# Later due times for layer-norm scalings in a planned graph kernel, and the last store in two pieces

## The chip, the cores and the metric

The kernel runs on one core of one Trainium2 chip. The metric is the device time of one execution in microseconds (us). A core has five engines that run side by side, each with its own in-order queue of instructions: TensorE (PE, matrix products), VectorE (DVE, elementwise work and statistics), ScalarE (ACT, activations and copies), GpSimd (POOL) and SyncE (SP, which here only issues transfers). They wait for one another through semaphores. Products land in PSUM banks, which PE writes and ACT and DVE read; everything else lies in SBUF or in DRAM.

## The reference, cut to what matters

Sixteen graphs (batches) of 1024 nodes with 128 features share one symmetric 0/1 adjacency matrix. Layer 0 is a graph attention, layer 1 five steps of a gated recurrent unit, and each ends with a residual and a layer norm:

```python
h = x @ others_weight                       # layer 0: attention
e = leaky(u1[:, idx1] + u2[:, idx2])
att = softmax(where(adj > 0, e, NEG_BIG), axis=1)
y = layernorm(x + att @ h + x @ self_weight)

h = y                                       # layer 1: five steps
for step in range(5):
    m = adj @ h                             # the reference takes it twice: m_in, m_out
    u3 = h @ u3_w.T + u3_b
    z = sigmoid([m, m] @ w3_w.T + w3_b + u3)
    r = sigmoid([m, m] @ w4_w.T + w4_b + u3)
    hv = tanh([m, m] @ w5_w.T + w5_b + (r * h) @ u5_w.T + u5_b)
    h = (1 - z) * h + z * hv
out = layernorm(y + h)
```

A layer norm subtracts the mean over the 128 features and divides by sqrt(variance + 1e-5).

## The kernel before, in words

The adjacency matrix stays in SBUF (`adj`), with four tables of sums of its quarters (`tab`). Batches are taken in pairs. `layer0(b)` computes the attention of one batch and its norm; the result `y0` is the start of layer 1 and is also put away in DRAM (`yd`) for the residual at the end. `messages(q, s, k)` multiplies the state of pair q by the adjacency matrix in step s. Where a step is in the list `PLAIN`, it does so with plain products (PE rows `ps_acc`); otherwise it needs seven products in place of eight, on sums of quarters (rows `ps_acc_a`, `ps_acc_c` and `gz` of line 621). The accumulated bank `ps_acc_a` is copied out by ACT between two products that go on adding to it (lines 1141 and 1143), so PE can't start the next one ahead of that copy. `gates(b, s, soon)` does the gates: u3 (L1189), a copy of it (L1192), r and z (L1199, and tanh on ACT, L1202), r times h (DVE, L1209), the candidate (L1215, L1216, tanh L1221), and the new h by three DVE instructions (L1224, L1227, L1230). Each batch's 1024 nodes are worked on in two halves, e or g = 0 and 1.

After a step, `leave(b, s)` turns h from feature-major to node-major: DVE transposes blocks of 32x32 (L579), SP sends the tile to DRAM with the blocks swapped (L589) and reads it back as `G` or `F` (L597). ACT and DVE then split it into a high and a low part (L609, L613). After the last step of batches 0 to 13 it adds the residual (L1332, into a tile of kind `o`, of which there are two), norms it in place, and POOL issues the store to the output (L1344). SP has loaded the residual into that tile before (L1324). The last two batches, 14 and 15, end in `end(b, s, g, h, rank)`: PE transposes h (L571), DVE adds the residual (L1262), and SP stores the result (L1278), half a batch at a time.

`layernorm(...)` has three parts. `look` is DVE's: statistics of four blocks of 128 features (L527, L529). `power` is POOL's: variance plus epsilon, to the power -0.5 (L533, L534), and the product with the mean (L539 and L540, or L542 and L543 for batches with the other sign). `scale` is ACT's: four activations of 128x128 with that scale and bias (L548). With `short=True`, which only batch 15's second half uses, POOL stops after the power (for this sign) and DVE scales (`scale_short`, L554). The norms of layer 0 are called `y`, those of layer 1 `o`, in the tile names too (`mv_y`, `rstd_o`).

Nothing of this is issued in the order of the source. Each piece of work is added to a `Plan` with its engine, a length in ns, a rank, and what it reads and writes. `Plan.order` then plays a list schedule: of the pieces that are ready on a free engine it takes the one with the lowest rank. A piece becomes ready when all that it depends on have ended in the plan, plus a lag; lengths on DVE and ACT are taken 1.1 times. The lag is set by the engine (200 ns for POOL) or by the piece itself. The order found so is the order in which instructions go into the engines' queues; on the chip each queue keeps it, and the semaphores do the rest. So a lag in the plan costs no time by itself: it moves the dependent instruction, and then whatever the plan finds to do in its place.

```python
plan.add("POOL", 2301 if short else 3001, rank, power, reads=[(mv, 0)], writes=[(rstd, 0)])
if short:
    dve(900, rank, scale_short, reads=[*after, (mv, 0), (rstd, 0)], writes=[write])
else:
    act(1250, rank, scale, reads=[*after, *later, (mv, 0), (rstd, 0)], writes=[write])
```

The argument `later` names further things that the scaling has to follow in the plan. Before, only batch 14's second half has one: the tanh result `hv` of batch 15, last step, second half.

Of the kernel before, what the change touches and what calls it, by code (L numbers as in the profile page):

```python
# [16 lines left out]
P = 128  # L17
# [3 lines left out]
STEPS = 5  # L21
# [116 lines left out]
def kernel(  # L138
# [79 lines left out]
    def exact(pools):  # L218
# [300 lines left out]
                dve(V, 1 + c / 4, sum_, reads=[*y, *more], writes=[(("tab",), c, n)])  # L519


        def layernorm(key, g, rank, after, src, dst, write, sg=1, short=False, later=()):
            stats, mv, rstd = ("stats", *key, g), ("mv", *key, g), ("rstd", *key, g)

            def look():
                for j in range(4):
                    nc.vector.bn_stats(T(stats)[:, j, :], src(j))  # L527
                for j in range(4):
                    nc.vector.bn_aggr(T(mv)[:, j, :], T(stats)[:, j, :])  # L529

            def power():
                mean, var, r = T(mv)[:, :, 0], T(mv)[:, :, 1], T(rstd)
                nc.gpsimd.tensor_scalar(r[:, 0, :], var, EPS, None, ALU.add)  # L533
                nc.gpsimd.tensor_tensor(r[:, 0, :], r[:, 0, :], mhalf[:, 0:4], ALU.pow)  # L534
                if short:
                    if sg < 0:
                        nc.gpsimd.tensor_scalar(r[:, 0, :], r[:, 0, :], -1.0, None, ALU.mult)
                elif sg > 0:
                    nc.gpsimd.tensor_scalar(r[:, 1, :], mean, -1.0, None, ALU.mult)  # L539
                    nc.gpsimd.tensor_tensor(r[:, 1, :], r[:, 1, :], r[:, 0, :], ALU.mult)  # L540
                else:
                    nc.gpsimd.tensor_tensor(r[:, 1, :], mean, r[:, 0, :], ALU.mult)  # L542
                    nc.gpsimd.tensor_scalar(r[:, 0, :], r[:, 0, :], -1.0, None, ALU.mult)  # L543

            def scale():
                r = T(rstd)
                for j in range(4):
                    nc.scalar.activation(  # L548
                        dst(j), src(j), AF.Identity, bias=r[:, 1, j : j + 1], scale=r[:, 0, j : j + 1]
                    )  # L550

            def scale_short():
                for j in range(4):
                    nc.vector.tensor_scalar(  # L554
                        dst(j), src(j), T(mv)[:, j, 0:1], T(rstd)[:, 0, j : j + 1], ALU.subtract, ALU.mult
                    )

            after = after if isinstance(after, list) else [after]
            dve(1100, rank, look, reads=after, writes=[(stats, 0), (mv, 0)])
            plan.add("POOL", 2301 if short else 3001, rank, power, reads=[(mv, 0)], writes=[(rstd, 0)])  # L560
            if short:
                dve(900, rank, scale_short, reads=[*after, (mv, 0), (rstd, 0)], writes=[write])
            else:
                act(1250, rank, scale, reads=[*after, *later, (mv, 0), (rstd, 0)], writes=[write])

# [65 lines left out]
        def layer0(b):  # L631
# [331 lines left out]
            for g in range(2):  # L963
                rank = rank0(b) + D["l5"]

                def y(g=g):
                    return T(yT[g])

                t = ("ps", "t", b, "y", g)
                if on_pe(b, "y"):  # L970
                    transposes(y, [(yT[g], 0)], t, rank)
                else:
                    k, d, t = (x + (b, "y", g) for x in (("T",), ("D",), ("F",)))
                    turn(k, y, [(yT[g], 0)], rank)
                    away(k, d, rank)
                    back(d, t, rank)

                def src(j, t=t, flat=on_pe(b, "y")):
                    return T(t)[:, j * P : (j + 1) * P] if flat else chunks(T(t))[:, j]

                def dst(j, g=g, flat=on_pe(b, "y")):
                    c = T(y0[g])[:, j, :]
                    return c if flat else c.rearrange("p (a j) -> p a j", a=4)

                layernorm(("y", b), g, rank0(b) + D["l6"], (t, 0), src, dst, (y0[g], 0), sign(b))

            if not plain(b // 2, 0):

# [256 lines left out]
        def end(b, s, g, h, rank):  # L1245

            hT, t = ("hT", b), ("ps", "t", b, s, g)
            o, yd = ("y0" if b == B - 1 else "o", b, "o", g), ("yd", b, g)
            sp(
                450,  # L1250
                rank,
                lambda: nc.sync.dma_start(T(o).rearrange("p c d -> p (c d)"), T(yd)),
                reads=[(yd, 0), (("m", b, s, 0), 0)],
                writes=[(o, "y")],
                lag=2300,
            )

            transposes(h, [(hT, g)], t, rank + D["tr"])

            def add_():  # L1260
                x = T(o).rearrange("p c d -> p (c d)")
                nc.vector.tensor_tensor(x, T(t), x, ALU.add)  # L1262

            dve(V, rank + D["o"], add_, reads=[(t, 0), (o, "y")], writes=[(o, "raw")])

            def src(j):
                return T(o)[:, j, :]

            def dst(j):
                return T(o)[:, j, :]  # L1270


            later = [(("hv", B - 1, STEPS - 1, 1), 0)] if (b, g) == (B - 2, 1) else []
            layernorm(("o", b), g, rank + D["ln"], (o, "raw"), src, dst, (o, 0), sign(b), b == B - 1 and g == 1, later)
            sp(
                450,
                rank + D["out"],
                lambda: nc.sync.dma_start(out[b].rearrange("(c p) d -> p c d", p=P)[:, 4 * g : 4 * g + 4, :], T(o)),  # L1278
                reads=[(o, 0)],
            )  # L1280

        def leave(b, s):

# [2 lines left out]
            for g in range(2):  # L1286

                def h(g=g):
                    return T(hT)[:, g * HALF : (g + 1) * HALF]

                k, d = ("T", b, s, g), ("X", b, s + 1, g)
                if s < STEPS - 1 and on_pe(b, s):
                    t = ("ps", "t", b, s, g)
                    transposes(h, [(hT, g)], t, rank + D["tr"])
                    split(
                        ("blk", b, "h", s + 1, g),
                        lambda t=t: T(t).rearrange("p (c a j) -> p c a j", c=4, a=4),
                        [(t, 0)],
                        rank_of(b, s + 1),
                    )  # L1300
                    continue
                if s < STEPS - 1:
                    turn(k, h, [(hT, g)], rank + D["tr"])
                    away(k, d, rank + D["tr"])
                    continue

                if b >= B - 2:
                    end(b, s, g, h, rank)
                    continue

                t = ("ps", "t", b, s, g)
                if on_pe(b, s):
                    transposes(h, [(hT, g)], t, rank + D["tr"])
                else:
                    t = ("F", b, s, g)
                    turn(k, h, [(hT, g)], rank + D["tr"])
                    away(k, d, rank + D["tr"])
                    back(d, t, rank + D["o"])

                o, yd = ("o", b, g), ("yd", b, g)  # L1320
                sp(
                    450,
                    rank + D["o"],
                    lambda o=o, yd=yd: nc.sync.dma_start(T(o).rearrange("p c d -> p (c d)"), T(yd)),  # L1324
                    reads=[(yd, 0), (hT, g)],
                    writes=[(o, "y")],
                )

                def last(t=t, o=o, flat=on_pe(b, s)):
                    x = T(o).rearrange("p c (a j) -> p c a j", a=4)  # L1330
                    n = T(t).rearrange("p (c a j) -> p c a j", c=4, a=4) if flat else chunks(T(t))
                    nc.vector.tensor_tensor(x, n, x, ALU.add)  # L1332

                dve(V, rank + D["o"], last, reads=[(t, 0), (o, "y")], writes=[(o, "raw")])

                def at(j, o=o):
                    return T(o)[:, j, :]

                layernorm(("o", b), g, rank + D["ln"], (o, "raw"), at, at, (o, 0), sign(b))
                plan.add(  # L1340
                    "POOL",
                    900,
                    rank + D["out"],
                    lambda o=o, g=g: nc.gpsimd.dma_start(  # L1344
                        out[b].rearrange("(c p) d -> p c d", p=P)[:, 4 * g : 4 * g + 4, :], T(o)
                    ),
                    reads=[(o, 0)],
                    writes=[((o, "sent"), 0)],
                    lag=2600,
                )  # L1350
# [347 lines left out]
```

## Time and profile before

| what | us |
|---|---|
| median of three runs | 1460.33 |
| lowest and highest run | 1458.93, 1460.43 |
| the profiled execution, its own time | 1468.01 |
| its span, first to last instruction | 1466.2 |
| PE not busy: up to 40 us | 3.1 |
| PE not busy: 100 to 200 us | 1.3 |
| PE not busy: 200 to 400 us | 4.4 |
| PE not busy: 400 to 600 us | 2.2 |
| PE not busy: 1200 to 1400 us | 1.3 |
| PE not busy: from 1440 us on | 14.4 of 27.0 |

The idle rows come from the view of busy time by stretches; the stretches that are left out have none. A row of the timeline gives start, duration, engine, line of the kernel, operation, tiles, shape, and in brackets the idle time of the engine before it with what ended that. Lines of the profile are lines of the kernel before. Busy times of PE are modelled ends of pipelined products, so one group's end overlaps the next one's start a little. In PE's rows a product of 32-bit numbers shows as two instructions.

### The profile page before, as it was taken

How to read it: one execution, taken by the hardware profiler on the slowest of the kernel's cores; microseconds unless marked ns; L12 is line 12 of the kernel's file. 1: busy time of each engine (PE TensorE's matmuls, PEld its weight loads, DVE VectorE, ACT ScalarE, POOL GpSimd, SP SyncE). 2: the span in 40 equal slices, each digit the busy share in tenths (PEclk: the TensorE clock that was granted, in tenths of full speed). 3: DMA queues.
4: the chain of work that ended last, by engine and by line, in shares of the span. 5: the costliest groups of instructions: out<-in, count | busy, mean ns of one | idle time of the engine just before them, and what ended most of it. 6: DMA issues, size and time to landing. Idle time of an engine off the chain costs nothing.

```text
span 1466.2 us, 17789 instructions
## 1 busy us (share of the span) xinstructions
PE 1440.4 (98%) x5020; PEld 902.3 (62%) x5020; DVE 1160.1 (79%) x2753; ACT 896.2 (61%) x1792; POOL 203.3 (14%) x323
## 2 busy tenths in 40 slices
PE   9999999998999999999999999999999999999996
PEld 7766656665566656666666656656566656556663
DVE  5997789868888789987888788896988877776535
ACT  5656465665657665666657576566655656664544
POOL 0311001012101150110201112011200123000201
PEclk9999999999999999999999999999999999999998
DMA  7426135554434643455434543445432554223201
GB/s 250 145 55 205 52 102 150 137 158 116 112 100 137 184 126 90 121 163 150 108 108 123 158 129 101 115 143 159 123 89 79 150 166 129 58 72 87 72 0 31
DMA packets 188032, 174.20 MB, mean 119 GB/s; under 512 B 34239, under 2 KB 137366, under 8 KB 187926
## 3 DMA queue, kind: packets, MB, share of 16 engines
q1 hardware_dynamic: 182562, 156.41, 37.8%
q0 software_dynamic: 4800, 15.73, 3.2%
q8 instruction: 41, 0.67, 0.2%
q10 hardware_dynamic: 564, 0.85, 0.2%
q14 instruction: 65, 0.53, 0.1%
HBM read 95.68 MB, written 77.24 MB: 118 GB/s over the span
## 4 chain that ended last, share of the span: by engine, by line
PE 88%; DVE 4%; DMA 2%; SPq 1%; ACT 1%; issue 1%; POOL 1%; DVEq 0%; POOLq 0%; ACTq 0%
PE ps_acc_a L621 16%; PE ps_g_r L1199 8%; PE ps_g_v L1215 8%; PE ps_g_v L1216 8%; PE gz L1199 8%; PE ps_g_r L1189 8%; PE ps_acc_c L621 8%; PE ps_acc_po L621 8%; PE ps_acc L621 5%; PE gz L621 4%; PE ps_g_ph L658 1%; PE ps_idle L419 1%; SPq L589 1%; PE ps_acc_px L925 1%; PE ps_acc_po L939 1%
## 5 line engine op out<-in xcount | busy, mean ns | idle before, releaser
L1215 PE MATMUL ps_g_v<-m,wm 128*128 128x512 f32 x320 | 163.5, 592 | 0.1
L1216 PE MATMUL ps_g_v<-r,u5h 128*128 128x512 f32 x320 | 163.4, 592 | 0.0
L1199 PE MATMUL ps_g_r<-m,wm 128*128 128x512 f32 x320 | 160.0, 593 | 2.6 <-ACT gz L1192 2.6
L1199 PE MATMUL gz<-m,wm 128*128 128x512 f32 x320 | 159.5, 592 | 0.0
L1189 PE MATMUL ps_g_r<-hT,u 128*128 128x512 f32 x320 | 153.3, 592 | 0.0
L1224 DVE TENSOR_TENSOR hv<-hv,hT 128x512 f32<-128x512 f32 x160 | 109.8, 686 | 51.5 <-ACT hv L1221 51.0
L621 PE MATMUL ps_acc_a<-tab,blk_s 128*128 128x512 f32 x544 | 148.6, 415 | 1.6 <-ACT m L1141 1.6
L1209 DVE SCALAR_TENSOR_TENSOR r<-r,hT 128x512 f32<-128x512 f32 x160 | 109.2, 685 | 51.3 <-ACT r L1202 51.0
L1202 ACT ACTIVATE r<-ps_g_r,bh 128x512 f32<-128x512 f32 x160 | 109.1, 687 | 66.4 <-PE ps_g_r L1199 66.1
L621 PE MATMUL ps_acc_po<-adj,blk 128*128 128x512 f32 x512 | 141.5, 423 | 0.0
L1202 ACT ACTIVATE z<-gz,bh 128x512 f32<-128x512 f32 x160 | 109.6, 687 | 24.5 <-PE gz L1199 24.0
L621 PEld LDWEIGHTS ps_acc_a<-tab,blk_s 128*128 128x128 f32 x544 | 101.1, 188 | 37.5 <-issue 11.1
L621 PEld LDWEIGHTS ps_acc_po<-adj,blk 128*128 128x128 f32 x512 | 95.9, 188 | 36.6 <-issue 12.5
L1230 DVE SCALAR_TENSOR_TENSOR hT<-hv,hT 128x512 f32<-128x512 f32 x160 | 108.7, 681 | 2.2
L1227 DVE SCALAR_TENSOR_TENSOR hv<-z,hv 128x512 f32<-128x512 f32 x160 | 108.4, 678 | 2.1 <-ACT z L1202 1.1
L1192 ACT COPY gz<-ps_g_r 128x512 f32<-128x512 f32 x160 | 91.0, 572 | 29.7 <-PE ps_g_r L1189 28.2
L533 POOL TENSOR_SCALAR rstd_y<-mv_y 128x4 f32<-128x4 f32 x32 | 13.5, 422 | 682.1 <-DVE mv_y L529 657.6
L1216 PEld LDWEIGHTS ps_g_v<-r,u5h 128*128 128x128 f32 x320 | 60.6, 189 | 76.8 <-issue 61.1
L1199 PEld LDWEIGHTS gz<-m,wm 128*128 128x128 f32 x320 | 60.5, 190 | 76.4 <-issue 76.4
L621 PE MATMUL ps_acc<-adj,blk_h 128*128 128x512 f32 x384 | 101.3, 414 | 0.0
L609 ACT CAST blk_s<-G 128x512 fp32r<-128x512 f32 x136 | 82.3, 617 | 30.8 <-DVE G L1083 29.2
L613 DVE TENSOR_TENSOR blk_s<-G,blk_s 128x512 fp32r<-128x512 f32 x136 | 92.0, 681 | 8.7 <-ACT blk_s L609 8.2
(191 smaller groups left out, 2595.4 us busy)
## 6 DMA issues: line engine op xcount, KB each, us to landing
G<-X SPq DMA_DIRECT2D x140, 256.0 KB, 2.9
X<-T SPq DMA_DIRECT2D x552, 64.0 KB, 1.8
yd<-y POOLq DMA_DIRECT2D x32, 256.0 KB, 3.3
D_y<-T_y SPq DMA_DIRECT2D x112, 64.0 KB, 1.8
F_y<-D_y SPq DMA_DIRECT2D x28, 256.0 KB, 2.7
X<-y SPq DMA_DIRECT2D x28, 256.0 KB, 2.0
D_b<-T_b SPq DMA_DIRECT2D x112, 64.0 KB, 2.2
F_b<-D_b SPq DMA_DIRECT2D x28, 256.0 KB, 3.0
```

The source lines that it names most:

```text
L613: lambda: nc.vector.tensor_tensor(half(1), src(), half(0), ALU.subtract),
L621: nc.tensor.matmul(T(bank), T(blk)[:, k, c, :], right(c), start=(first and i == 0), stop=(last and i == len(terms) - 1), skip_group_check= ...
L1189: nc.tensor.matmul(T(pr), u3, h(), start=True, stop=True)
L1192: nc.scalar.copy(T(pz), T(pr))
L1199: nc.tensor.matmul(T(p_), wm[:, j, :], T(m), start=False, stop=True, skip_group_check=True)
L1202: nc.scalar.activation(T(t), T(p_), AF.Tanh, bias=bh[:, j : j + 1], scale=0.5 * sg)
L1209: lambda r=r, h=h: nc.vector.scalar_tensor_tensor(T(r), T(r), 1.0, h(), ALU.add, ALU.mult),
L1215: nc.tensor.matmul(T(pv), wm[:, 2, :], T(m), start=True, stop=False)
L1216: nc.tensor.matmul(T(pv), u5h, T(r), start=False, stop=True)
L1224: nc.vector.tensor_tensor(T(hv), T(hv), h(), ALU.subtract)
L1227: nc.vector.scalar_tensor_tensor(T(hv), T(z), 1.0, T(hv), ALU.add, ALU.mult)
L1230: nc.vector.scalar_tensor_tensor(h(), T(hv), 0.5, h(), ALU.mult, ALU.add)
```

## The change

It has four parts.

1. `layernorm` takes an argument `calm`, which it hands to the plan as the lag of POOL's power. For the `y` norms it is 1201 ns for batches 4 to 15; for the `o` norms of batches 0 to 13 (in `leave`) 4001 ns. Elsewhere it stays None, which means 200 ns.
2. `later` now holds for both halves of batch 14: the first half's scaling follows the tanh of batch 15's first half in the plan, the second half's that of the second half.
3. `scale_short` is cut into two pieces of two instructions each, every one a piece of the plan of its own.
4. The last store (batch 15, second half) becomes two of 128 KB each: ACT's queue issues the first, SP's queue the second, each after its own piece of the scaling.

Ranks (`D` and the rest) are the same in both kernels. Numbers and kinds of instructions are the same too, but for one more transfer on ACT's queue, as the last store is two.

```diff
-        def layernorm(key, g, rank, after, src, dst, write, sg=1, short=False, later=()):
+        def layernorm(key, g, rank, after, src, dst, write, sg=1, short=False, later=(), calm=None):
...
-            def scale_short():
-                for j in range(4):
+            def scale_short(js):
+                for j in js:
...
-            plan.add("POOL", 2301 if short else 3001, rank, power, reads=[(mv, 0)], writes=[(rstd, 0)])
+            plan.add(
+                "POOL", 2301 if short else 3001, rank, power, reads=[(mv, 0)], writes=[(rstd, 0)], lag=calm
+            )
             if short:
-                dve(900, rank, scale_short, reads=[*after, (mv, 0), (rstd, 0)], writes=[write])
+                for i in range(2):
+                    js = range(2 * i, 2 * i + 2)
+                    dve(
+                        510,
+                        rank,
+                        lambda js=js: scale_short(js),
+                        reads=[*after, (mv, 0), (rstd, 0)],
+                        writes=[(write[0], i)],
+                    )
...
-                layernorm(("y", b), g, rank0(b) + D["l6"], (t, 0), src, dst, (y0[g], 0), sign(b))
+                layernorm(("y", b), g, rank0(b) + D["l6"], (t, 0), src, dst, (y0[g], 0), sign(b), calm=1201 if b >= 4 else None)
...
-            later = [(("hv", B - 1, STEPS - 1, 1), 0)] if (b, g) == (B - 2, 1) else []
+            later = [(("hv", B - 1, STEPS - 1, g), 0)] if b == B - 2 else []
...
-            sp(
-                450,
-                rank + D["out"],
-                lambda: nc.sync.dma_start(out[b].rearrange("(c p) d -> p c d", p=P)[:, 4 * g : 4 * g + 4, :], T(o)),
-                reads=[(o, 0)],
-            )
+            view = out[b].rearrange("(c p) d -> p c d", p=P)[:, 4 * g : 4 * g + 4, :]
+            if (b, g) == (B - 1, 1):
+                for i, (add, by) in enumerate(((act, nc.scalar), (sp, nc.sync))):
+                    cs = slice(2 * i, 2 * i + 2)
+                    add(450, rank + D["out"], lambda by=by, cs=cs: by.dma_start(view[:, cs], T(o)[:, cs]), reads=[(o, i)])
+            else:
+                sp(450, rank + D["out"], lambda: nc.sync.dma_start(view, T(o)), reads=[(o, 0)])
...
-                layernorm(("o", b), g, rank + D["ln"], (o, "raw"), at, at, (o, 0), sign(b))
+                layernorm(("o", b), g, rank + D["ln"], (o, "raw"), at, at, (o, 0), sign(b), calm=4001)
```

## The prediction

> **What bounds the kernel now.** I read the head of the page first, then the waits of TensorE (PE), then the timeline around the longest of these waits, then busy time by stretches, and last the timeline of the final 20 us.
>
> ```profile
> span 1466.2 us, 17789 instructions
> PE 1440.4 (98%) x5020; PEld 902.3 (62%) x5020; DVE 1160.1 (79%) x2753; ACT 896.2 (61%) x1792; POOL 203.3 (14%) x323
> ```
>
> PE is busy 98% of the span, and the change leaves each of its instructions in place by kind and number. So only the 26 us in which PE is not busy can be won, and any new idle time of PE is lost. Who makes PE wait (total, times, longest, in us):
>
> ```profile
> PE ps_acc_a L621 <- ACT m L1143: 4.4, 1, 4.4
> PE ps_t L571 <- DVE hT L1230: 3.0, 3, 1.5
> PE ps_g_r L1199 <- ACT gz L1192: 2.6, 2, 1.7
> ...
> PE ps_acc_a L621 <- ACT m L1141: 1.6, 2, 1.1
> ```
>
> The L571 row belongs almost wholly to the end of the kernel. The three rows that name ACT are single events. The largest, in the timeline (start, duration, engine, line, operation; in brackets the idle time before it and its releaser):
>
> ```profile
> 332.12 1.27 DVE L613 TENSOR_TENSOR blk_x<-G,blk_x 128x512 fp32r<-128x512 f32 x2
> ...
> 332.30 4.78 POOL L533 TENSOR_SCALAR rstd_o<-mv_o 128x4 f32<-128x4 f32 x1 [29.03 <-DVE mv_o L529]
> ...
> 336.91 0.71 DVE L579 STREAM_TRANSPOSE T<-hT 128x512 f32<-128x512 f32 x1
> ...
> 338.57 0.24 POOL L543 TENSOR_SCALAR rstd_o<-rstd_o 128x4 f32<-128x4 f32 x1
> 338.85 1.65 ACT L548 ACTIVATE o<-o,rstd_o 128x128 f32<-128x128 f32 x4 [5.46 <-POOL rstd_o L543]
> ...
> 340.97 0.58 ACT L1143 ACTIVATE m<-ps_acc_a 128x512 f32<-128x512 f32 x1
> ...
> 341.60 3.59 PE L621 MATMUL ps_acc_a<-tab,blk_x 128*128 128x512 f32 x8 [4.37 <-ACT m L1143]
> ```
>
> The power of a layer norm (POOL, L533 to L543) is ready 6.6 us after its statistics (331.84+0.37 to 338.57+0.24). The planner had reckoned 3.0 + 0.2 us, so it had put the scaling L548 early in ACT's queue; ACT stands there 5.46 us, the copy L1143 is queued behind it, and PE waits for that copy. POOL's timeline shows two more slow L533: 4.18 us at 521.63 (ACT then idles 3.45 us, PE 1.72 us) and 2.99 us at 538.74 (PE 0.52 us at 547.2). Its shortest is 0.215 us. The stall costs more than its length:
>
> ```profile
> 330.00:337.20 7.20, 7.20 (x24) 3.84 (x22) 6.84 (x18) 2.27 (x4) 4.81 (x2) 1.00 0.20 50
> 337.20:341.60 4.40, 0.03 (x1) 0.00 (x0) 1.01 (x3) 2.75 (x7) 2.26 (x4) 1.00 0.47 151
> 341.60:345.30 3.70, 3.70 (x9) 2.92 (x10) 3.63 (x10) 1.24 (x4) 0.04 (x1) 0.54 0.29 84
> ```
>
> The last column but two is PE's granted clock. After the stall it is 0.54: the eight products at 341.60 take 3.59 us, where groups of eight in the chain of waits take 1.86. That is 1.7 us more.
>
> **What the Trainium skill says.** "SBUF — State Buffer", section "Who interferes with whom": a DVE instruction with two inputs in SBUF and a GpSimd instruction that reads SBUF contend for one port pair, and the loser blocks. The trace agrees and goes further: L533 starts at 332.30, sits through the eight two-input DVE instructions from 332.12 on, and ends just after the one-input transpose L579 begins. The two others also end with such a transpose. "TensorE: Matmul & The Clock Gate", Part 1: an idle window of about 3.4 us halves the clock. The trace agrees: 0.54 after 4.37 us, and no such stretch after the stall of 1.72 us. "DMA: Bandwidth & Descriptors", section "Issuing engines are not separate DMA queues": a second issuing engine saves only issue time. The trace can't test that.
>
> **The change part by part.**
>
> *Powers reckoned later.* For the `o` norms of batches 0 to 13 the planner now reckons 3.0+4.0 = 7.0 us, for the `y` norms of batches 4 to 15 3.0+1.2 = 4.2. This adds no instruction; it moves L548 back in ACT's queue, and with it everything planned after. I compared the emitted orders: PE's is the same up to about 260 us, different until about 1383 us, and the same again after. I anchored ACT's and DVE's instructions to PE's order, since PE hardly ever waits. The three scalings that stalled then stand 6.9, 1.6 and 11 us of PE work further behind their statistics, and none of these statistics is followed directly by a two-input DVE instruction any more (before: eight, seven, five). So I expect all three stalls gone: 4.37+1.7 (clock), 1.72, 0.52; sum 8.3 us. From below: the second may survive in part. The covers: ACT is 61% busy and has other work to put in place of the scaling; a store waits for its scaling (63.2 us on POOL, all hidden) and is sent up to 4 us later. On POOL a power queued behind such a store waits with it; on SP the load L1324 waits for the store that frees its `o` buffer (48.8 us in total, up to 8.2), with the transfers L589 and L597 behind it. The planner has moved these too, so I take 0, up to 2 us if not.
>
> *New stalls.* Before, I count 15 powers with five or more two-input DVE instructions right behind their statistics; three came late. After there are 13, so about 13×3/15 = 2.6 that come late. Eight of the 13 are `o` norms, nearly all covered by 7.0 us (slowest seen 6.7). Five are `y` norms: about one slow. The worst new one is that of batch 8, second half: eight such instructions at 0.60 us each plus the 1.8 us for the rest gives 6.6 us against 4.2, so ACT is up to 2.4 us late. PE lost 4.37, 1.72 and 0.52 of 5.46, 3.45 and 4.49 us that ACT lost, so about half: 1.2. With small stalls of other kinds (1.10 at 1205.9 is there now) I add 1.5 us; from 0 to 6.
>
> *Both scalings by the last tanhs.*
>
> ```profile
> 1447.25 1.64 ACT L548 ACTIVATE o_o<-o_o,rstd_o 128x128 f32<-128x128 f32 x4
> ...
> 1449.36 0.67 ACT L1221 ACTIVATE hv<-ps_g_v,b 128x512 f32<-128x512 f32 x1
> ...
> 1450.95 0.69 ACT L1221 ACTIVATE hv<-ps_g_v,b 128x512 f32<-128x512 f32 x1 [0.93 <-PE ps_g_v L1216]
> ...
> 1459.67 1.12 DVE L554 TENSOR_SCALAR y_o<-y_o,mv_o,rstd_o 128x128 f32<-128x128 f32 x4 [1.72 <-POOL rstd_o L534]
> 1459.91 1.43 SPq L1278 DMA_DIRECT2D out_dram<-y_o  x2
> ```
>
> The first half's scaling moves from ahead of the first tanh to between the two. The first tanh's bank is ready at 1449.20 (1448.18+1.02), so it gains at most 0.12. The second starts at about 1449.87+1.5 = 1451.4 in place of 1450.95, 0.4 late; but DVE reaches its result only at 1452.19 (now 1452.07), and the tanh then ends at 1452.09. Sum: -0.1, at worst +0.4. The second half's scaling stays behind both tanhs. Stores of batch 14 go out before 1454 and are hidden.
>
> *Last store in two.* The same four L554; after the second (about 1460.25) ACT can send 128 KB, 0.55 us before SP's store at 1460.81; after the fourth SP sends the rest. One more DMA on ACT: behind it are only ACT's flag load (0.46 us) and branch. The DMA view of the last 8 us shows data flowing at 260 to 300 GB/s from 1460.8 to 1463.2 with one dip to 123, so the gain is the dip and a shorter tail: -0.2; from -0.9 (all of issue and dip) to +0.4 (a further queue to wait for).
>
> **Sum.** Against the profiled execution (1468.01: span 1466.2 and 1.8 around it): -8.3 + 1.5 - 0.1 - 0.2 = -7.1, giving 1460.9. The median of the runs is 1460.33, 7.7 us below that execution. PE's work is the same in each, so some of its idle time may be missing from ordinary runs: between all of the 6.8 us net and nothing may count there. I take two thirds, because the DVE runs that block POOL lie in the program's order, while how far DVE lags behind depends on the landing of data (3.33 us of waiting for F before this one). So -4.5 - 0.3 = -4.8: **1455.5**.
>
> **Rivals.**
> *A, forecast*: 1455.5; 0.55. Within it 0.47 faster, 0.08 same.
> *B, the stalls are the profiled execution's own*: the 7.7 us speak for it, the lock's fixed order against it. Left are 0.3 from the end and some 0.5 of small stalls: 1459.5; 0.22 (0.19 same, 0.02 faster, 0.01 slower).
> *C, slower*: the lock moves to `y` norms that are reckoned at only 4.2 us, at batch 6 and batch 8, second halves. Seven and eight two-input instructions make ACT 1.8 and 2.4 us late with L1141 copies behind; if PE loses all 4.2 us and one clock window (1.7), that is 5.9. If the old stalls are worth only 1.3 in ordinary runs: 1460.3-1.3-0.3+5.9 = 1464.6; 0.15. It decides from where the new stalls exceed what the old ones really cost. For it: the runs of DVE work. Against: five `y` norms stood so before, none stalled PE.
> *D, a clean order*: all 8.3 gone and no new stall: 1452; 0.08.
>
> Differences under about 0.2% (2.9 us) can't be told from none. Faster 0.47+0.02+0.08 = 0.57, same 0.27, slower 0.16. Range 1451 (all gone, 8.3+0.3 and a little more) to 1463.5 (most of C left out).
>
> **What would show it.** Right: no PE wait for ACT L1143 above 1 us; no half clock between 50 and 1440 us; scalings L548 of `o` that hardly wait for POOL even behind an L533 of 4 us; the second tanh at about 1451.4; the last two stores starting some 0.55 us apart. Wrong: a `y` scaling on which ACT waits over 2 us with a PE gap behind it, PE gaps that sum to over 9 us, or SP waiting longer for `o` stores with PE gaps behind. If the profiled execution falls by 7 and the median hardly, B holds.

## The result, and the profile after

| what | us |
|---|---|
| before, median of 12 runs on the same chip | 1460.54 (1457.91 to 1463.18) |
| after, median of 12 runs | 1455.66 (1454.42 to 1459.33) |
| after / before | 0.9971, interval 0.9961 to 0.9981 |
| profiled execution before: its time, its span | 1468.01, 1466.2 |
| profiled execution after: its time, its span | 1459.33, 1457.2 |

The change makes the kernel faster by 0.29%, 4.9 us by the medians; the prediction was 1455.5. The profiled execution after is the highest of its twelve runs, the one before lies above all twelve. So both pages show an execution with more idle time than usual, and the pair has to be read with that in mind. In the one after, the extra time lies at the start: its first u3 product starts at 80.21 us, that of the run `both` below at 77.14.

The head of the page after:

```profile
span 1457.2 us, 17798 instructions
PE 1437.5 (99%) x5020; PEld 901.6 (62%) x5020; DVE 1161.3 (80%) x2753; ACT 897.1 (62%) x1792; POOL 194.8 (13%) x323
```

The work is the same. The span is 9.0 us shorter, and the time in which PE isn't busy is 19.7 us, where it was 25.8; the other 2.9 us are busy time of PE, which fell from 1440.4 to 1437.5. (In the table of idle time before, the last row counts 0.8 us past the end of the span.) (The lines of the kernel after are those of before plus 10 or 11 from line 562 on.) The waits of PE after, total, times and longest in us:

```profile
PE ps_t L581 <- DVE hT L1240: 2.8, 2, 1.5
PE ps_ahead L455 <- DMA r_x<-in_x_dram: 2.2, 1, 2.2
PE gz_fill L423 <- POOL ones L389: 1.4, 1, 1.4
PE ps_g_r L1209 <- ACT gz L1202: 1.1, 1, 1.1
```

All three rows that named ACT before, 4.4, 2.6 and 1.6 us, are gone or down to one event of 1.1. By their times the first row here is the end of the kernel and the next two its start. Between 150 and 1430 us PE has no wait at all in this view.

The same place as in the prediction, batch 0's norm, first half, in the timeline after:

```profile
338.77 0.36 DVE L529 BATCH_NORM_AGGREGATE mv_o<-stats_o 128x2 f32<-128x6 f32 x4
...
339.24 0.22 POOL L533 TENSOR_SCALAR rstd_o<-mv_o 128x4 f32<-128x4 f32 x1 [19.82 <-DVE mv_o L529]
...
341.10 0.55 POOL L543 TENSOR_SCALAR rstd_o<-rstd_o 128x4 f32<-128x4 f32 x1
...
347.11 1.65 ACT L548 ACTIVATE o<-o,rstd_o 128x128 f32<-128x128 f32 x4
```

The power is ready at 341.65 and the scaling starts at 347.11, 5.5 us later, without a wait: the lag is in the queue's order, as meant. Over all 28 such norms the scaling has 1.85 to 6.9 us in hand, and ACT has no wait for an `o` power of batches 0 to 13 (before: 20.5 us in 13 times). And the longest L533 is 0.706 us here, in the view of one tile (count, then ns least, median and most, first and last start):

```profile
L533 POOL TENSOR_SCALAR rstd_o<-mv_o x32: 215/560/706, 339.2 to 1449.3; 128x4 f32<-128x4 f32 x32
```

So no L533 was held up for long in this execution. The slowest of the 28 powers was ready 4.6 us after its statistics, and four took longer than the 3.2 us that the planner reckoned before: little of the room was needed.

The last 17 us:

```profile
1440.33 0.69 ACT L1231 ACTIVATE hv<-ps_g_v,b 128x512 f32<-128x512 f32 x1 [1.03 <-PE ps_g_v L1226]
1440.91 1.64 ACT L548 ACTIVATE o_o<-o_o,rstd_o 128x128 f32<-128x128 f32 x4
...
1442.45 0.67 ACT L1231 ACTIVATE hv<-ps_g_v,b 128x512 f32<-128x512 f32 x1
...
1443.18 0.69 DVE L1234 TENSOR_TENSOR hv<-hv,hT 128x512 f32<-128x512 f32 x1
...
1450.65 1.12 DVE L554 TENSOR_SCALAR y_o<-y_o,mv_o,rstd_o 128x128 f32<-128x128 f32 x4 [1.72 <-POOL rstd_o L534]
...
1451.29 0.41 ACTq L1289 DMA_DIRECT2D out_dram<-y_o  x1
1451.79 1.16 SPq L1289 DMA_DIRECT2D out_dram<-y_o  x1
```

Against the same copy of ACT just ahead (L1192 at 1443.16, now L1202 at 1434.25, so 8.91 us are taken off before comparing) the first tanh is 0.12 us earlier, the second 0.41 later, DVE 0.10 earlier, and the scaling L554 0.11 earlier. ACT's store goes out 0.50 us ahead of SP's, but SP's issue now takes 1.16 us where it took 0.53 before (1459.91+1.43-1460.81). From the start of L554 to the end of the span it is 6.57 us before and 6.52 after in the traces. Over all the runs below it is 6.42 to 6.91 with the end as before and 6.29 to 7.03 with the store in two, so no gain shows.

### The profile page after: what moved, and what is told of

It is laid out like the page before. It is cut to its first block, busy times and chain, and to the rows that moved or that the text cites. A ratio compares the mean times of both kernels' runs of the same rounds, so it can differ in the third digit from the quotient of the medians.

```text
span 1457.2 us, 17798 instructions
## 1 busy us (share of the span) xinstructions
PE 1437.5 (99%) x5020; PEld 901.6 (62%) x5020; DVE 1161.3 (80%) x2753; ACT 897.1 (62%) x1792; POOL 194.8 (13%) x323
## 4 chain that ended last, share of the span: by engine, by line
PE 97%; DMA 2%; DVE 1%; ACT 0%; issue 0%; SPq 0%; POOL 0%; POOLq 0%; DVEq 0%; ACTq 0%
PE ps_acc_a L631 17%; PE ps_g_r L1209 9%; PE ps_g_r L1199 9%; PE gz L1209 9%; PE ps_g_v L1225 9%; PE ps_g_v L1226 9%; PE ps_acc_c L631 9%; PE ps_acc_po L631 8%; PE ps_acc L631 6%; PE gz L631 4%; PE ps_g_ph L668 2%; PE ps_acc_px L935 1%; PE ps_acc_po L949 1%; PE ps_t L581 1%; DMA blk_boot<-in_adj_dram 1%; DMA hT_boot<-in_L_gnn_w_w_dram 1%
## 5 line engine op out<-in xcount | busy, mean ns | idle before, releaser
L1199 PE MATMUL ps_g_r<-hT,u 128*128 128x512 f32 x320 | 153.1, 592 | 0.0
L631 PE MATMUL ps_acc_po<-adj,blk 128*128 128x512 f32 x512 | 138.1, 417 | 0.0
L1202 ACT COPY gz<-ps_g_r 128x512 f32<-128x512 f32 x160 | 91.1, 572 | 33.2 <-PE ps_g_r L1199 31.7
L533 POOL TENSOR_SCALAR rstd_y<-mv_y 128x4 f32<-128x4 f32 x32 | 12.7, 397 | 660.6 <-DVE mv_y L529 660.2
```

The source lines that it names most:

```text
L631: nc.tensor.matmul(T(bank), T(blk)[:, k, c, :], right(c), start=(first and i == 0), stop=(last and i == len(terms) - 1), skip_group_check= ...
L1199: nc.tensor.matmul(T(pr), u3, h(), start=True, stop=True)
L1202: nc.scalar.copy(T(pz), T(pr))
```

## The experiments

To compare executions without start and end, I use the first and the last start of PE's u3 products (L1189, L1199 in the kernel after) and call what lies between them the middle. It is 1364.6 us before and 1354.3 after in the two profiled executions, with 9.16 and 1.59 us of PE idle. Ratios are to the kernel before on the same chip, of which there were three. The median there was 1460.12 us (27 runs) for `again`, `o_only`, `tail_only` and `pause`; 1461.14 (52) for `y_only`, `both` and the lags of 3501 and 1501; 1461.33 (39) for the lag of 4501, the spare powers and the third profile. The diffs show the lines that matter: where a lag is set, `layernorm` takes `calm` and hands it on as in the change, and the making of spare tiles is left out.

### The kernel before, profiled again (`again`)

No edit.

> The kernel before, unchanged, profiled once more. If the stalls belong to the order of the DVE queue (theory), this execution has them again: an L533 of over 3 us at the norms of batches 0, 2 and 3, and PE gaps for ACT of 4 to 8 us in sum. If they were an accident of that one profiled execution (rival B of the prediction), no L533 is over 1 us and the gaps between 150 and 1440 us sum to under 3 us.

Measured: 1458.91 us, span 1457.1, middle 1357.0, PE idle in it 3.15. The place of the L533 of 4.78 us, with DVE's instructions in the same order:

```profile
329.91 1.26 DVE L613 TENSOR_TENSOR blk_x<-G,blk_x 128x512 fp32r<-128x512 f32 x2
330.09 0.57 POOL L533 TENSOR_SCALAR rstd_o<-mv_o 128x4 f32<-128x4 f32 x1 [28.65 <-DVE mv_o L529]
...
330.74 1.34 POOL L534 TENSOR_TENSOR rstd_o<-rstd_o,mhalf 128x4 f32<-128x4 f32 x1
...
332.52 0.55 POOL L543 TENSOR_SCALAR rstd_o<-rstd_o 128x4 f32<-128x4 f32 x1
...
333.11 1.65 ACT L548 ACTIVATE o<-o,rstd_o 128x128 f32<-128x128 f32 x4 [2.05 <-POOL rstd_o L543]
```

L533 starts, as before, with L613 under way and seven more two-input instructions behind it. This time it is through after the first, in 0.57 us, ACT waits 2.05 and PE 0.22. What stays late is batch 3's second half (2.98 us), with batch 4's first (2.37) and batch 8's second (2.97) new. So in these executions the order decides which powers can be shut out, and chance which of them are. PE's largest loss here has nothing to do with powers:

```profile
1195.26 0.62 ACT L1037 COPY hT<-F_b 128x512 f32<-128x512 f32 x1 [4.35 <-DMA F_b<-D_b]
...
1195.78 0.58 ACT L1141 COPY m<-ps_acc_a 128x512 f32<-128x512 f32 x1
...
1196.41 0.96 PE L621 MATMUL ps_acc_a<-tab,blk_s 128*128 128x512 f32 x3 [1.55 <-ACT m L1141]
```

ACT stands 4.35 us at a copy whose data are still on their way, and the copy that PE needs is behind it.

### One part at a time

The `o` lag alone (`o_only`):

```diff
-                layernorm(("o", b), g, rank + D["ln"], (o, "raw"), at, at, (o, 0), sign(b))
+                layernorm(("o", b), g, rank + D["ln"], (o, "raw"), at, at, (o, 0), sign(b), calm=4001)
```

> The kernel before with the later lag for the o norms alone (4001 ns); y norms and the end as before. Theory (the late o powers are what costs): 3.5 to 4.7 us less than before, about 1456.3, and no scaling of o that waits over 1 us for POOL. Rival (the y lag or the end brings the gain): within 1.5 us of before.

Measured: 1461.20 us (1458.97 to 1463.45), ratio 1.0006 [0.9995, 1.0016]. ACT's waits for these powers are gone from its profile, though one L533 took 3.58 us in it, and the time is that of before. Its middle is 1358.7 us with 3.72 of PE idle, for other things. PE's longest waits from 100 to 1430 us:

```profile
PE ps_g_r L1199 <- ACT gz L1192: 1.3, 2, 0.8
PE ps_acc_a L621 <- ACT blk_x L609: 0.8, 1, 0.8
PE ps_g_ph L658 <- ACT hv L1221: 0.6, 1, 0.6
```

The stalls that I had priced don't carry the gain by themselves.

The end alone (`tail_only`: both `later`, the cut scaling, the two stores; no lag):

```diff
-            later = [(("hv", B - 1, STEPS - 1, 1), 0)] if (b, g) == (B - 2, 1) else []
+            later = [(("hv", B - 1, STEPS - 1, g), 0)] if b == B - 2 else []
...
+                for i, (add, by) in enumerate(((act, nc.scalar), (sp, nc.sync))):
```

> The end of the changed kernel alone: both scalings of batch 14 after the tanhs, last scaling and last store in two, no later lags. Theory: 0.1 to 0.4 us less than before, so no difference that can be measured; the three late L533 are still there in the profile. Rival (the end brings the gain): 3 us or more less.

Measured: 1460.72 us, ratio 1.0000 [0.9987, 1.0013]. No more than a microsecond or two can be in it, and the timeline has 0.1. In its trace PE, DVE and POOL go through the same sequence of operations and tiles as before, and ACT too up to the last 20 us, so it is one more execution of that order: middle 1357.1 us, idle 3.62, and two late L533, those of batch 3's and batch 8's second halves (2.98 and 2.97 us), where I had expected all three of the first profile.

The `y` lag alone (`y_only`):

```diff
-                layernorm(("y", b), g, rank0(b) + D["l6"], (t, 0), src, dst, (y0[g], 0), sign(b))
+                layernorm(("y", b), g, rank0(b) + D["l6"], (t, 0), src, dst, (y0[g], 0), sign(b), calm=1201 if b >= 4 else None)
```

> The kernel before with the later lag for the y norms of batches 4 to 15 alone (1201 ns). Theory 1, room (each lag takes away waits for POOL): no y power was late enough to stop PE before, so within 1 us of before. Theory 2, the draw (any new lag gives a new order of everything from 260 us on, and orders differ by some us whatever the lag says): anything from 3 us less to 3 us more.

Measured: 1460.94 us (1456.55 to 1465.0), ratio 0.9998 [0.9987, 1.0010]. Nothing either.

Both lags, with the end as before (`both`: the diffs of `o_only` and `y_only` together):

> Both later lags as in the changed kernel, with the end as before. If the lags carry the gain: 4 to 5 us less than before, within 0.7 us of the changed kernel (1455.7). If the end does its part only together with them: half of that or less.

Measured: 1455.71 us (1454.83 to 1456.56), ratio 0.9962 [0.9948, 0.9976]; middle 1354.2, idle 1.52. This is the whole change but for its end, and it has the whole gain. Two lags that are worth nothing each are worth 5 us together. If the gain were the waits for late powers, the `o` lag alone, which leaves ACT 2.5 us of waits for `y` powers and none for the `o` powers in question, would have had most of it. So I put the gain down to the new order that the two lags give together; which part of that order brings it isn't shown.

### Taking away what shuts POOL out (`pause`)

Two spare statistics on DVE after each norm's own, into a tile that nobody reads, so that no two-input instruction stands right behind them. All orders are those of before.

```diff
+                for j in range(2):
+                    nc.vector.bn_stats(spare[:, j, :], src(j))
```

> The kernel before with every order as it was, but two spare bn_stats of 128 features (one input each, results unused) on DVE after each norm's statistics, 64 times about 0.4 us of added DVE work. If DVE instructions with two inputs in SBUF shut POOL out (theory), L533 gets in during the spare ones: no L533 over 1 us, the three stalls of PE gone, 3 to 5 us less than before although the kernel does more. If the stalls come from elsewhere (POOL itself, or the order as such): the same time or 1 to 3 us more.

Measured: 1478.75 us, ratio 1.0129 [1.0109, 1.0150]: 18 us slower where I had expected 3 to 5 less. The timeline at batch 0 says why:

```profile
330.92 0.46 DVE L532 BATCH_NORM_STATS2 spare<-o 128x6 f32<-128x128 f32 x2
...
331.09 0.23 POOL L536 TENSOR_SCALAR rstd_o<-mv_o 128x4 f32<-128x4 f32 x1 [28.26 <-DVE mv_o L530]
...
331.40 5.68 POOL L537 TENSOR_TENSOR rstd_o<-rstd_o,mhalf 128x4 f32<-128x4 f32 x1
...
336.09 0.71 DVE L582 STREAM_TRANSPOSE T<-hT 128x512 f32<-128x512 f32 x1
...
337.80 1.65 ACT L551 ACTIVATE o<-o,rstd_o 128x128 f32<-128x128 f32 x4 [5.60 <-POOL rstd_o L546]
...
340.56 0.80 PE L624 MATMUL ps_acc_a<-tab,blk_x 128*128 128x512 f32 x1 [4.03 <-ACT m L1146]
```

The variance plus epsilon, now L536, gets through in 0.23 us, as I had wanted (0.68 at most over all 32). The next POOL instruction, the power itself, meets the same run of DVE work and is shut out for most of 5.68 us: it ends at 337.08, and its shortest duration is 1.04, so it gets in about when the transpose begins. It isn't the only one: 18 of the 64 powers L537 took over 2 us, where before none of the 64 did. The lock had only been handed on. DVE's added work, 23.5 us more busy time (1183.6 against 1160.1), comes on top; which share of the 18 us is whose wasn't separated.

### Other values of the lags

Each value gives the planner other due times, and so an order of its own from about 260 us on. All three are the kernel after with one number changed.

```diff
-                layernorm(("o", b), g, rank + D["ln"], (o, "raw"), at, at, (o, 0), sign(b), calm=4001)
+                layernorm(("o", b), g, rank + D["ln"], (o, "raw"), at, at, (o, 0), sign(b), calm=3501)
```

> The changed kernel with 3501 ns in place of 4001 for the o norms. Theory 1, room: 6.5 us reckoned is still ahead of nearly every power, so within 1 us of 1455.7. Theory 2, the draw: the order is another one, so the time can lie anywhere between 1455 and 1462, and PE gaps for ACT copies appear at places that have no late power.

Measured: 1457.97 us, ratio 0.9977 [0.9968, 0.9986].

```diff
-... calm=1201 if b >= 4 else None)
+... calm=1501 if b >= 4 else None)
```

> The changed kernel with 1501 ns in place of 1201 for the y norms. Theory 1, room: more room, so 1455.7 or up to 0.7 us less. Theory 2, the draw: anywhere between 1455 and 1462, with PE gaps at places that have no late power.

Measured: 1458.80 us, ratio 0.9989 [0.9979, 0.9998].

```diff
-... (o, 0), sign(b), calm=4001)
+... (o, 0), sign(b), calm=4501)
```

> The changed kernel with 4501 ns in place of 4001 for the o norms: one more order that has both lags. Room says 1455 to 1457, the draw 1455 to 1462. The two before it came out at 1458.0 and 1458.8, so I expect 1457.5.

Measured: 1463.11 us (1461.43 to 1467.49), ratio 1.0014 [1.0005, 1.0024]: slower than before, with more room reckoned than after. Again ACT never waits for an `o` power of batches 0 to 13, not even for one whose L533 took 4.18 us. PE's waits in its middle (100 to 1430 us):

```profile
PE ps_g_r L1209 <- ACT gz L1202: 2.1, 3, 1.4
PE ps_g_ph L668 <- ACT hv L1231: 1.1, 1, 1.1
PE ps_t L581 <- DVE hT L1240: 0.9, 1, 0.9
PE ps_g_v L1226 <- DVE r L1219: 0.8, 1, 0.8
```

The second row, followed back in the timeline:

```profile
1020.35 0.69 DVE L1343 TENSOR_TENSOR o<-F,o 128x512 f32<-128x512 f32 x1 [2.52 <-DMA o<-yd]
...
1022.62 0.66 DVE L1240 SCALAR_TENSOR_TENSOR hT<-hv,hT 128x512 f32<-128x512 f32 x1
...
1023.37 0.69 ACT L1231 ACTIVATE hv<-ps_g_v,b 128x512 f32<-128x512 f32 x1 [3.81 <-DVE hT L1240]
...
1024.11 0.60 PE L668 MATMUL ps_g_ph<-wo,xt 128*128 128x131 f32 x3 [1.09 <-ACT hv L1231]
```

DVE stands at the residual's addition because the residual isn't loaded yet; the new h behind it comes late, then the tanh, then PE's product. The load was late in SP's queue:

```profile
1015.22 0.86 SPq L1335 DMA_DIRECT2D o<-yd  x2
```

The data are there 5.1 us later. In the kernel after, the same load goes out at 1010.71 and DVE doesn't wait for it. No store is in its way: the last one from an `o` tile had been issued at 895.73, over 100 us before. The two other long waits of this kind in the middle, 5.27 us at 847 and 3.03 at 1195, are alike, each with the first load of a pair of batches some 5 us ahead of its use. So here it is the order on SP that costs. DVE's waits for this load in whole executions, total, times and longest:

```profile
DVE o L1343 <- DMA o<-yd: 17.9, 7, 5.3
```

In the kernel after the row is smaller:

```profile
DVE o L1343 <- DMA o<-yd: 7.6, 2, 6.6
```

It is 7.0, 6.6 and 5.7 us in the three calm executions of the order before (`again`, the third profile, `tail_only`), 7.7 with both lags, 8.4 with 3501 and 23.0 with 1501. With 1501 a wait of 6.94 us at 1225.60 lies ahead of PE's largest gap, 1.74 at 1231, though there ACT stands for a `G` load as well. That load went out at 1222.61, right after a store from an `o` tile had landed, so there a later scaling can be the reason: it delays its store, the store frees one of the two `o` tiles, and the load waits for that. A third `o` tile wasn't tried.

### Lateness put in by hand (`late_before`, `late_both`)

Two spare powers of some 1.1 us each in POOL's work for the 28 `o` norms, into a tile that nobody reads, unknown to the planner; first with the orders of before, then with both lags.

```diff
+                for _ in range(2 if key[0] == "o" and key[1] < B - 2 else 0):
+                    nc.gpsimd.tensor_tensor(spare, r[:, 0, :], mhalf[:, 0:4], ALU.pow)
```

> The kernel before in its own order, with two spare powers (results unused, about 1.1 us each) in POOL's work for each of the 28 o norms of batches 0 to 13: every o scale is ready about 2.2 us later. In the profile of before 13 of the 28 scalings follow their power by 0.04 us and 11 more by under 2.2 us, so ACT waits some 40 us more. Theory 1, room: PE loses at least a quarter of that, 10 us or more. If POOL's lateness doesn't reach PE: under 2 us more.

Measured: 1487.61 us, ratio 1.0178 [1.0149, 1.0208].

> Both later lags, the end as before, and the same two spare powers for the 28 o norms. In the profile of the changed kernel the scalings of o follow their power by 1.85 to 6.9 us, so 2.2 us more stay inside nearly everywhere. Theory 1, room: within 1.5 us of the same order without them (1455.7). Theory 2, only the draw of the order matters: it loses about as much as the kernel before does with them.

Measured: 1457.23 us (1455.19 to 1460.99), ratio 0.9982 [0.9972, 0.9992]. ACT's waits, first with the orders of before:

```profile
ACT o L551 <- POOL rstd_o L543: 37.5, 12, 6.7
...
ACT o L551 <- POOL rstd_o L546: 26.3, 13, 4.1
```

Then with both lags:

```profile
ACT o L551 <- POOL rstd_o L543: 0.8, 2, 0.6
```

Two spare powers for each norm cost 26 us without the lags and 1.5 with them by the medians (1457.23 over the 1455.71 of `both`, which ran on another chip), some 3 by the ratios. In the first run PE idles 21.68 us in the middle, and its clock is halved four times there, for 3.41 us each. The lateness wasn't quite the same: of 56 spare powers the slowest took 4.70 us in the first run and 2.17 in the second. But the difference is far larger than that, and it is the room that the change makes: 63.8 us of waiting against 0.8.

### The kernel before, a third time (`again2`)

No edit.

> The kernel before, unchanged, a third profiled execution. If how long L533 is held up is chance from one execution to the next, late ones come at other norms than in the two before (batches 0, 2, 3 and then 3, 4, 8), except that of batch 3, second half, which came in both with 2.98 us; the time from the first L1189 to the last differs by over 1 us from at least one of them.

Measured: 1458.79 us, span 1457.0, middle 1356.7, PE idle in it 3.16. Only batch 3's second half is late:

```profile
L533 POOL TENSOR_SCALAR rstd_o<-mv_o x32: 215/520/2986, 330.2 to 1448.9; 128x4 f32<-128x4 f32 x32
```

The wait for `F_b` at 1196 is there again (PE 0.96 us). The stall of 4.37 us and the stretch at half clock behind it are not.

## Why the prediction was right or wrong

- **The number** was right: 1455.5 against 1455.66, and faster, as forecast. Much of that is luck: a term of the sum failed and the rest made up for it, and the `o` lag, which was to bring nearly all of the gain, brings none by itself.
- **What bounds the kernel** was right in the main: PE is busy 1440.4 us before, 1437.5 after and 1436.2 in both later profiles of the kernel before. But not all that was won is idle time, as the prediction had it. In the middle PE's time without the idle time is 1353.4 to 1353.8 us in the three calm executions of the order before, and 1352.6 and 1352.7 with the lags.
- **The three stalls, 8.3 us.** In the profiled pair they went as predicted, and the half clock in the middle with them. But two of the three belonged to that one execution: in the three later ones of its order PE idles 3.15, 3.16 and 3.62 us in the middle, not 9.16.
- **The step that failed** is the share kept for ordinary runs: "I take two thirds, because the DVE runs that block POOL lie in the program's order". The order does lie in the program, and one power, batch 3's second half, was late in each of the four executions (2.99, 2.98, 2.99 and 2.98 us). But the same order let batch 0's power through in 0.57 us, and PE lost 9.16 us in the middle once and 3.15 to 3.62 three times. Rival B was right on what it said of the stalls, and wrong that nothing else would change.
- **New stalls, 1.5 us.** Measured: none after 142 us. Rival C's place, `y` powers of batches 6 and 8, stayed quiet in the profile: no L533 above 0.71 us.
- **What replaced these terms.** From the executions of the order before without the large stall (middle 1357.0, 1356.7 and 1357.1) to the lags (1354.2 and 1354.3) there are 2.7 us. Of these 1.8 are idle time, some of it no power at all, like the 1.55 and 0.96 us at the `F_b` copy, which the new order doesn't have; 0.9 are PE's busy time, and why it is shorter wasn't looked for. The rest of the 4.9 us may be lateness by chance that reaches PE in an ordinary run: the medians of before beside two calm executions lie 1.2 and 2.5 us above them (1460.12 over 1458.91, 1461.33 over 1458.79). The spread doesn't speak for that: the twelve runs of each kernel on one chip reach over 5.3 us before and 4.9 after. This division is argued, not shown.
- **What stays open** is how much of the gain is room and how much the draw of an order. Room is real, as the spare powers show. But four pairs of lags that all give room are 1455.7, 1458.0, 1458.8 and 1463.1 us, a span wider than the gain; and each lag alone gives nothing. One part of the draw is known: where the residual's load comes to stand.
- **That load** was in the prediction, on SP, "0, up to 2 us if not". For this change 0 held: PE lost nothing to it. For 4501 it didn't, though there the load was late in SP's own order and not behind a store.
- **The tanhs** were right to a few hundredths: predicted 0.12 at most, 0.4 and 0.1; measured 0.12, 0.41 and 0.10.
- **The store in two** was mis-sized: -0.2 predicted, -0.05 measured, and nothing that stands out from other executions. "DMA: Bandwidth & Descriptors" of the Trainium skill, section "Issuing engines are not separate DMA queues", says that only issue time is saved; here ACT's issue lies 0.50 us ahead of SP's, and the end doesn't come sooner by that.
- **The lock.** "SBUF — State Buffer" of the Trainium skill, section "Who interferes with whom", has the loser blocked for the other's instruction. The traces agree that a two-input DVE instruction blocks POOL and that a transpose, with one input, lets it in. They show two things beside: the loser can stay blocked through eight of them, and needn't.

## What to carry to other kernels

A lag in a planner acts by a new order of everything after it, so measure a few values and the parts alone before its gain is put down to the wait it was meant for. Profile the kernel before more than once ahead of pricing a stall; what comes back in each execution belongs to the order, the rest to chance. Whether a schedule has room is best asked by putting the lateness in by hand: two spare powers for each norm cost 26 us in the one order and 1.5 to 3 in the other.

## What the runs showed that was not expected

- One POOL instruction of 0.22 us took 0.57 or 4.78 us behind the same eight DVE instructions, which follow one another every 0.60 us. It was shut out until a one-input instruction began, or it slipped in after the first.
- Letting that instruction through moved the block to the next one (5.68 us, where 1.04 is the shortest), and the kernel was 18 us slower, with DVE busy 80% of the span.
- The half clock needs no wait of 4.37 us, nor of the 3.4 us that the prediction cites: PE waited 2.24 us up to 28.75 at the start of the kernel after, and ran at half clock for 3.41 us from 30.55 on. In the middle of `late_before` waits of 3.11, 2.73, 3.32 and 3.12 us were each followed by half clock, and one of 2.33 us wasn't.
- SP's issue of the last store took 1.16 us in the kernel after and 1.12 in `tail_only`, but 0.37, 0.37 and 0.52 in the three other runs with the same end, and 0.37 to 0.78 in those where SP issues both. So ACT's issue just ahead isn't the reason; what is, stays open.
